# One block transpose for both heads, and row sums inverted by a power on GpSimd, in a four-layer attention kernel

## The chip, the core and the metric

The kernel runs on one core of a Trainium2 chip. The metric is the device time of one launch in microseconds (us), the median of several runs. One further execution was recorded by the hardware profiler; its trace gives the times of single instructions. The engines are PE (TensorE, matrix products), PEld (its weight loads), DVE (VectorE), ACT (ScalarE), POOL (GpSimd) and SP (SyncE, which here only issues DMAs). Each engine works through its own queue in order and waits on semaphores for the others.

## The reference

Two sequences of 1024 rows of 128 numbers run through eight residual blocks. Four of them are attention with 16 heads of 64, and they are what matters here:

```python
def attention(x):                        # x: (2, 1024, 128), after a layer norm
    s = q @ k.T / 8                      # per head, 1024 x 1024; three of the four are causal
    w = softmax(s, axis=-1)              # exp(s - rowmax) / rowsum
    return (w @ v) @ w_o
# layer a: one k and v for all heads, no mask;  b: causal;
# c: causal, k and v from a latent of 32;       d: causal, with biases
x = x + a(norm(x)); x = x + ffn(norm(x))
x = x + b(norm(x)); x = x + ffn(norm(x))
x = x + c(norm(x)); x = x + moe(norm(x))
x = x + d(norm(x)); x = x + moe(norm(x))
```

`ffn` is one dense product with its input rounded to a small grid, `moe` a small mixture of eight experts with two chosen for each row. Everything is float32.

## The kernel before, in words

A **unit** is one layer, one sequence and one pair of heads: 4 x 2 x 8 = 64 units. A unit is done in **steps**, each for one or two query tiles of 128 rows, chosen so that a step has at most 1024 columns of scores for each head. Layer a has no mask: eight steps, one query tile with 1024 keys each (`FULL_STEPS`, L587). The causal layers have five: query tiles 7, then 6 with 0, 5 with 1, 4 with 2, and 3 (`CAUSAL_STEPS`, L588). In all there are 128 + 3 x 80 = 368 steps.

For one step, in the order of the computation:

- `scores` (L623): PE multiplies queries by keys for both heads into PSUM (`sc`, two buffers, one for each head); DVE takes the negated row maximum of each head and query tile (`nmax`, L682).
- `exponentials` (L688): ACT writes exp(score - max) into the tile `pr` and the row sums into `tot` (L693). The tile `pr` has two buffers.
- `normalize` (L698): DVE takes the reciprocal of the row sums, one instruction of 128x2 or 128x4 (`rec`, L701). POOL multiplies the probabilities by it in place, one instruction for each head and query tile (L705).
- `transposes` (L761): the probabilities must be transposed for the product with the values. Most key tiles are transposed by DVE in 32x32 blocks, one instruction for each head and query tile (L775), into the tile `slots`. Key tiles outside a "blocked" range go through PE (`pp`, L792) and a copy on ACT (L793): in layer a the last key tile, in the others query tiles 0 to 3.
- `blocks_moved` (L736): when two neighbouring query tiles are done, the 32-partition blocks are moved to their places in `prT` by 16 DMAs issued on SP (L750). In layer a 13 are DMAs, two are copies on POOL (L754) and one a copy on ACT.
- `weigh` (L804): PE multiplies the transposed probabilities by the values (`av`, L849 and L844), ACT copies the result, PE multiplies by the output weights (`po`, L870), ACT copies it, and POOL adds it into x (L893).

The main loop (L1089) is a software pipeline written by hand; every engine gets its instructions in the order in which this loop emits them. In the iteration of step n it emits first the transposes of step n - 2. The normalising of step n - 1 is emitted after the first part of these transposes:

```python
            for _ in transposes(st):
                if last_step:
                    normalize(last_step.pop())
```

`transposes` is a generator, and a part ends at each `yield`. So DVE's queue before the change holds: transpose of head 0 (step n - 2), reciprocal (step n - 1), transpose of head 1 (step n - 2), then the maxima of step n. After that the iteration emits the additions into x, the scores, maxima and exponentials of step n, parts of the next unit's projections and of other work (layer norms, feed-forward blocks, as `side`), and four parts of `weigh`. A block of probabilities is used by `weigh` at the earliest two steps after its moves were emitted (L1131).

Where the tile `pr` lies in memory: before, it is [128, 2, 1024], so each head's columns are contiguous.

Of the kernel before, what the change touches and what calls it, by code (L numbers as in the profile page):

```python
# [9 lines left out]
F32 = mybir.dt.float32  # L10
BF16 = mybir.dt.bfloat16
I32 = mybir.dt.int32
AF = mybir.ActivationFunctionType
ALU = mybir.AluOpType
# [3 lines left out]
P = 128  # L18
B, S, D = 2, 1024, 128
NT = S // P  # L20
H, DH = 16, 64
NPAIR = H // 2
QB = 512
NQB = S // QB
# [3 lines left out]
TPA = AB // P  # L28
# [8 lines left out]
def kernel(ctx: ExitStack, tc: tile.TileContext, a: dict, out: bass.AP):  # L37
    nc = tc.nc

    const = ctx.enter_context(tc.tile_pool(name="const", bufs=1))  # L40
# [18 lines left out]
    for b in range(B):  # L59
        xb = xpool.tile([P, NT, D], F32, tag=f"x{b}", name=f"x{b}")  # L60
        for g in range(NT // TPB):
            nc.sync.dma_start(
                out=xb[:, g * TPB : (g + 1) * TPB, :],
# [42 lines left out]
    prT_four = probTp.tile([P, 2 * 4 * AB], F32, tag="prT_four", name="prT_four")  # L106
    latT_first = probTp.tile([P, S], F32, tag="latT", name="latT")


    stats = {}  # L110

# [149 lines left out]
    def moe_group(nm, b, g, last, xT, eng=nc.gpsimd, other=None):  # L261
# [3 lines left out]
        if other:  # L265
            xn = qkp.tile([P, TPB, D], F32, tag="qx", name=f"xn_{k}")
            hids = [
                probp.tile([P, 2, S], F32, tag="pr", name=f"hid_{k}_{n}").rearrange(
                    "p h (c q) -> p (h c) q", q=QB
                ) for n in range(2)  # L270
            ]
        else:
            xn = None
# [335 lines left out]
    def keys(u, qt):  # L609
        return qt + 1 if layers[u[0]]["causal"] else NT  # L610

    def step_of(u, qts):
        k = f"{tag_of(u)}_{qts[0]}"
        at = {}
        if len(qts) == 2:
            at = {qts[1]: 0, qts[0]: keys(u, qts[1]) * P}
        else:
            at = {qts[0]: QB - min(QB, keys(u, qts[0]) * P // 2)}
        pr = probp.tile([P, 2, S], F32, tag="pr", name=f"pr_{k}")
        tot = small.tile([P, 2, len(qts)], F32, tag="tot", name=f"tot_{k}")  # L620
        return dict(u=u, qts=qts, at=at, k=k, pr=pr, tot=tot)

    def scores(st):  # L623
# [61 lines left out]
            nmaxs.append(nmax)  # L685
        return sc, nmaxs

    def exponentials(st, h, sc, nmax):  # L688

        u, tot = st["u"], st["tot"]  # L690
        for n, qt in enumerate(st["qts"]):
            c = slice(st["at"][qt], st["at"][qt] + keys(u, qt) * P)
            nc.scalar.activation(  # L693
                st["pr"][:, h, c], sc[:, c], AF.Exp, bias=nmax[:, n : n + 1],
                accum_out=tot[:, h, n : n + 1],
            )

    def normalize(st):  # L698
        u, pr = st["u"], st["pr"]
        rec = small.tile([P, 2, len(st["qts"])], F32, tag="rec", name=f"rec_{st['k']}")  # L700
        nc.vector.reciprocal(out=rec, in_=st["tot"])  # L701
        for h in range(2):
            for n, qt in enumerate(st["qts"]):
                c = slice(st["at"][qt], st["at"][qt] + keys(u, qt) * P)
                nc.gpsimd.tensor_scalar(  # L705
                    out=pr[:, h, c], in0=pr[:, h, c], scalar1=rec[:, h, n : n + 1], scalar2=1.0,
                    op0=ALU.mult, op1=ALU.mult,
                )

# [26 lines left out]
    def blocks_moved(u, qb):  # L736


        t, src = prT_of(u, qb)[:, : 2 * blocked(u, qb) * AB], blocks_of(u, qb)
        n = src.shape[1] // 4  # L740
        def ends(i, r):
            return t[QUARTERS[r], i * n : (i + 1) * n], src[QUARTERS[i], r * n : (r + 1) * n]

        copied = (1, 2, 3) if layers[u[0]]["kind"] == "shared" else ()
        for i, r in MOVES:
            if i != r or i not in copied:
                o, x = ends(i, r)
                nc.sync.dma_start(out=o, in_=x)  # L750
        for i in copied:
            o, x = ends(i, i)
            if i < 3:
                nc.gpsimd.tensor_scalar(  # L754
                    out=o, in0=x, scalar1=1.0, scalar2=1.0, op0=ALU.mult, op1=ALU.mult
                )
            else:
                copies.append((o, x))
        probT[u, qb] = t.rearrange("p (i t h c) -> p t h i c", t=TPA, h=2, i=4)

    def transposes(st):  # L761

        u, pr = st["u"], st["pr"]
        for qt in st["qts"]:
            qb, cols = qt // TPA, slice(qt % TPA * P, (qt % TPA + 1) * P)
            nk, nb = keys(u, qt), blocked(u, qb)
            for h in range(2 if nb else 0):
                n = min(nk, nb)  # L770
                dst = blocks_of(u, qb).rearrange(
                    "p (r t h k q) -> p t h k r q", r=4, t=TPA, h=2, q=32
                )[:, qt % TPA, h, :n]
                src = pr[:, h, st["at"][qt] : st["at"][qt] + n * P]
                nc.vector.transpose(  # L775
                    dst,
                    src.rearrange("p (k r q) -> p k r q", r=4, q=32),
                )
                yield
            if nb < nk and nb:  # L780
                o = rest_of(u, qb)[:, qt % TPA].unsqueeze(2)
            elif nb < nk:
                if (u, qb) not in probT:
                    probT[u, qb] = prT_of(u, qb).rearrange("p (h k q) -> p h k q", h=2, q=AB)
                o = probT[u, qb][:, :, :, cols]
            for k0 in range(nb, nk, 2):
                k1 = min(k0 + 2, nk)
                pt = ps_m.tile([P, 2, 2, P], F32, tag="pm", name=f"pp_{tag_of(u)}_{qt}_{k0}")
                for h in range(2):
                    for kt in range(k0, k1):  # L790
                        c0 = st["at"][qt] + kt * P
                        nc.tensor.transpose(pt[:, h, kt - k0, :], pr[:, h, c0 : c0 + P], ident)  # L792
                nc.scalar.copy(o[:, :, k0 - nb : k1 - nb], pt[:, :, : k1 - k0, :])  # L793
                yield
            complete[u, qb] = complete.get((u, qb), 0) + 1
            if nb and complete[u, qb] == TPA:
                blocks_moved(u, qb)
# [6 lines left out]
    def weigh(u, qb, bank, kt, ends):  # L804


        li, b, p = u
        causal = layers[li]["causal"]
        nkt = keys(u, (qb + 1) * TPA - 1)
        n, nb = bank.index(qb), len(bank)  # L810
        if kt == 0 and n == 0:
            pv_of[u] = ps_av.tile([P, 2, AB], F32, tag="av", name=f"av_{tag_of(u)}_{qb}")
        av = pv_of[u]

        t0 = max(0, kt - qb * TPA) if causal else 0

        def moving(h, kt, t0, t1=TPA):
            if not blocked(u, qb):
                return probT[u, qb][:, h, kt, t0 * P : t1 * P]
            if kt >= blocked(u, qb):  # L820
                return rest_of(u, qb)[:, :, h]
            x = probT[u, qb][:, t0, h] if t1 - t0 == 1 else probT[u, qb][:, :, h]
            cols = slice(kt * 32, (kt + 1) * 32)
            return x[:, :, cols] if t1 - t0 == 1 else x[:, :, :, cols]

        def shaped(o, t0, t1=TPA):
            if not blocked(u, qb):
                return o[:, t0 * P : t1 * P]
            if kt >= blocked(u, qb):
                return o.rearrange("p (t q) -> p t q", t=TPA)  # L830
            if t1 - t0 == 1:
                return o[:, t0 * P : t1 * P].rearrange("p (i q) -> p i q", q=32)
            return o.rearrange("p (t i q) -> p t i q", t=TPA, q=32)

        for h in range(2):
            if layers[li]["kind"] == "latent":

                o = av[QUARTERS[2 * h + kt % 2], n]
                if kt == 1 and t0:
                    nc.tensor.matmul(  # L840
                        shaped(o, 0, t0), lhsT=zeros, rhs=moving(h, 0, 0, t0),
                        start=True, stop=True,
                    )
                nc.tensor.matmul(  # L844
                    shaped(o, t0), lhsT=vs[u][:, kt, :], rhs=moving(h, kt, t0), start=(kt < 2),
                    stop=(kt >= nkt - 2),
                )
            else:
                nc.tensor.matmul(  # L849
                    shaped(av[ROWS[h], n], t0), lhsT=vs[u][:, kt, h, :], rhs=moving(h, kt, t0),  # L850
                    start=(kt == 0), stop=(kt == nkt - 1),
                )
        if ends:
            o = attp.tile([P, 2, AB], F32, tag="at", name=f"attnT_{tag_of(u)}_{qb}")
            if layers[li]["kind"] == "bias":
                nc.scalar.activation(
                    o[:, :nb], av[:, :nb], AF.Identity, bias=b_v[:, p : p + 1]
                )
            else:
                nc.scalar.copy(o[:, :nb], av[:, :nb])  # L860
            outs.append((u, bank, o))
# [371 lines left out]
```

## Time and profile before

| what | value |
|---|---|
| time, median of 3 runs | 2314.12 us (2311.34 to 2315.66) |
| the profiled execution: span from its first to its last instruction | 2309.5 us |
| mean granted PE clock in it | 0.969 |
| instructions | 43436 |
| DVE block transposes (L775), count and length | 640; 0.83 us for 640 elements to 1.23 us for 1024 |
| DVE reciprocals (L701) | 368; 0.15 to 0.17 us |
| POOL normalising products (L705) | 1024; 0.38 us for 128 elements to 1.12 us for 1024 |
| layers a, b, c, d in the span | 24 to 690, 690 to 1188, 1188 to 1677, 1677 to 2235 us |
| one step of layer a, on average | 5.16 us |

The profiled execution has no time of its own beside its span; the runs' median is 4.6 us above that span.

How to read the lines that follow: a group or a timeline row names the source line, the engine and the operation, then output <- input with the name of the tile (`sc_a` is the scores of layer a). A row of waits names who waited for whom, the total in us, how many times, and the longest. A table of stretches gives, for each, its length and the busy time of PE, PEld, DVE, ACT and POOL with the number of instructions. The chain that ended last is followed back from the last instruction to what released it, step by step; its shares tell on which engine the time went along that chain.

### The profile page before, as it was taken

The page shows a single profiled execution, that of the slowest core. Times are in us where ns is not written, and L with a number is a line of the kernel's source. Part 1 is how long each engine was busy: PE and PEld are TensorE (multiplying, and loading weights), DVE is VectorE, ACT ScalarE, POOL GpSimd, SP SyncE. Part 2 cuts the span into 40 slices and gives each one's busy share as a digit, 9 for nine tenths or more (in the row PEclk, how much of TensorE's full clock was granted, in tenths as well). Part 3 has the DMA queues.
Part 4 walks back from the last instruction along what each step waited for, and adds up shares of the span by engine and source line. Part 5 has one row for each costly group of instructions (what it writes and reads, how often), then busy time and mean ns, then how long its engine had stood idle before and what let it go on. Part 6 is the DMA issues. An engine that isn't in the chain of part 4 may idle for free.

```text
span 2309.5 us, 43436 instructions
## 1 busy us (share of the span) xinstructions
PE 2112.7 (91%) x14833; PEld 1232.0 (53%) x14833; DVE 1716.0 (74%) x2695; ACT 1491.3 (65%) x3340; POOL 1285.7 (56%) x1723
## 2 busy tenths in 40 slices
PE   6999999999998999999987897888889999999986
PEld 2454444444445666666654454444455666656653
DVE  7978999999986876678668877776666566766544
ACT  5777777767765666666665566656666557666552
POOL 4756767767765454455545645555644446544441
PEclk9999999999999999999998889899899999999997
DMA  5666666556676666666655556544665546646450
GB/s 139 145 150 151 154 150 149 135 131 153 149 189 153 151 154 161 164 153 156 150 130 121 121 128 146 130 104 111 162 156 131 125 114 156 162 118 145 110 135 10
DMA packets 144635, 320.45 MB, mean 139 GB/s; under 512 B 48288, under 2 KB 58784, under 8 KB 144416
## 3 DMA queue, kind: packets, MB, share of 16 engines
q1 hardware_dynamic: 144416, 317.67, 58.2%
q8 instruction: 120, 1.97, 0.4%
q14 instruction: 99, 0.81, 0.1%
HBM read 10.27 MB, written 2.10 MB: 5 GB/s over the span
## 4 chain that ended last, share of the span: by engine, by line
PE 49%; DVE 15%; SPq 12%; ACT 10%; DMA 5%; issue 5%; POOL 3%; DVEq 0%; ACTq 0%; POOLq 0%
SPq L750 12%; PE sc_a L638 5%; PE av_a L849 4%; PE av_d L849 4%; DVE slots L775 4%; DMA prT<-slots 4%; PE sc_b L638 4%; PE av_b L849 4%; PE sc_d L638 4%; DVE nmax_a L682 3%; ACT pr_a L693 3%; ACT pr_c L693 3%; PE sc_c L638 3%; DVE nmax_d L682 2%; DVE nmax_c L682 2%
## 5 line engine op out<-in xcount | busy, mean ns | idle before, releaser
L693 ACT ACTIVATE pr_a<-sc_a,nmax_a 128x1024 f32<-128x1024 f32 x256 | 283.2, 1111 | 169.9 <-DVE nmax_a L682 168.0
L705 POOL TENSOR_SCALAR pr_a<-pr_a,rec_a 128x1024 f32<-128x1024 f32 x256 | 284.1, 1123 | 192.9 <-DVE rec_a L701 192.6
L705 POOL TENSOR_SCALAR pr_d<-pr_d,rec_d 128x1024 f32<-128x1024 f32 (+7 forms) x256 | 186.9, 750 | 269.0 <-DVE rec_d L701 268.8
L682 DVE TENSOR_REDUCE nmax_a<-sc_a 128x1 f32<-128x1024 f32 x256 | 298.3, 1204 | 28.0 <-PE sc_a L638 27.6
L705 POOL TENSOR_SCALAR pr_b<-pr_b,rec_b 128x1024 f32<-128x1024 f32 (+7 forms) x256 | 187.3, 752 | 219.9 <-DVE rec_b L701 219.5
L705 POOL TENSOR_SCALAR pr_c<-pr_c,rec_c 128x1024 f32<-128x1024 f32 (+7 forms) x256 | 187.5, 753 | 206.4 <-DVE rec_c L701 206.4
L682 DVE TENSOR_REDUCE nmax_d<-sc_d 128x1 f32<-128x1024 f32 (+7 forms) x256 | 177.1, 747 | 150.2 <-PE sc_d L644 150.2
L693 ACT ACTIVATE pr_c<-sc_c,nmax_c 128x1024 f32<-128x1024 f32 (+7 forms) x256 | 186.5, 739 | 153.5 <-DVE nmax_c L682 123.9
L693 ACT ACTIVATE pr_b<-sc_b,nmax_b 128x1024 f32<-128x1024 f32 (+7 forms) x256 | 186.5, 739 | 146.8 <-DVE nmax_b L682 130.3
L638 PE MATMUL sc_a<-k_a,q_a 64*128 64x512 f32 x512 | 266.8, 631 | 15.0 <-ACT pr_a L693 14.2
L775 DVE STREAM_TRANSPOSE slots<-pr_a 128x896 f32<-128x896 f32 x256 | 278.8, 1093 | 1.7 <-DMA prT<-slots 1.3
L693 ACT ACTIVATE pr_d<-sc_d,nmax_d 128x1024 f32<-128x1024 f32 (+7 forms) x256 | 186.6, 739 | 135.0 <-DVE nmax_d L682 129.5
L638 PE MATMUL sc_a<-k_a,qx_a 64*128 64x512 f32 x512 | 264.1, 631 | 0.0
L682 DVE TENSOR_REDUCE nmax_b<-sc_b 128x1 f32<-128x1024 f32 (+7 forms) x256 | 176.6, 745 | 89.0 <-PE sc_b L644 88.9
L682 DVE TENSOR_REDUCE nmax_c<-sc_c 128x1 f32<-128x1024 f32 (+7 forms) x256 | 176.8, 747 | 84.8 <-PE sc_c L653 84.0
L849 PE MATMUL av_a<-prT,v_a 128*64 128x256 f32 x1792 | 221.4, 386 | 7.5 <-DMA prT<-slots 5.2
L849 PEld LDWEIGHTS av_a<-prT,v_a 128*64 128x64 f32 x1792 | 121.1, 136 | 122.3 <-issue 69.0
L638 PE MATMUL sc_d<-k_d,q_d 64*128 64x512 f32 (+3 forms) x416 | 159.9, 497 | 0.3 <-ACT pr_d L693 0.3
L638 PE MATMUL sc_b<-k_b,q_b 64*128 64x512 f32 (+3 forms) x416 | 159.1, 495 | 1.1 <-ACT pr_b L693 1.1
L638 PE MATMUL sc_d<-kx_d,qx_d 64*128 64x512 f32 (+3 forms) x416 | 154.3, 490 | 0.2
L638 PE MATMUL sc_b<-kx_b,qx_b 64*128 64x512 f32 (+3 forms) x416 | 153.5, 488 | 0.7 <-ACT pr_b L693 0.6
L775 DVE STREAM_TRANSPOSE slots<-pr_b 128x1024 f32<-128x1024 f32 (+3 forms) x128 | 130.5, 1024 | 9.6 <-DMA prT<-slots 9.0
(408 smaller groups left out, 4782.3 us busy)
## 6 DMA issues: line engine op xcount, KB each, us to landing
prT<-slots SPq DMA_DIRECT2D x768, 128.0 KB, 2.3
prT<-slots SPq DMA_DIRECT2D x832, 112.0 KB, 2.2
prT<-slots SPq DMA_DIRECT2D x768, 96.0 KB, 2.1
qx_b<-q_b SPq DMA_DIRECT2D x32, 256.0 KB, 3.5
kx_b<-k_b SPq DMA_DIRECT2D x32, 256.0 KB, 3.4
qx_d<-q_d SPq DMA_DIRECT2D x32, 256.0 KB, 3.6
kx_d<-k_d SPq DMA_DIRECT2D x32, 256.0 KB, 3.5
x<-in_x SPq DMA_DIRECT2D x4, 256.0 KB, 3.7
```

Source lines behind the costliest of these rows:

```text
L638: yield nc.tensor.matmul(sc[h][:, at[qt] + k0 : at[qt] + k1], lhsT=q[r, qt * P : (qt + 1) * P], rhs=kk[r, k0:k1], start=True, stop=not dia ...
L682: nc.vector.tensor_reduce(out=nmax[:, n : n + 1], in_=sc[h][:, c], axis=AX.X, op=ALU.max, negate=True)
L693: nc.scalar.activation(st["pr"][:, h, c], sc[:, c], AF.Exp, bias=nmax[:, n : n + 1], accum_out=tot[:, h, n : n + 1],)
L705: nc.gpsimd.tensor_scalar(out=pr[:, h, c], in0=pr[:, h, c], scalar1=rec[:, h, n : n + 1], scalar2=1.0, op0=ALU.mult, op1=ALU.mult,)
L750: nc.sync.dma_start(out=o, in_=x)
L775: nc.vector.transpose(dst, src.rearrange("p (k r q) -> p k r q", r=4, q=32),)
L849: nc.tensor.matmul(shaped(av[ROWS[h], n], t0), lhsT=vs[u][:, kt, h, :], rhs=moving(h, kt, t0), start=(kt == 0), stop=(kt == nkt - 1),)
```

## The change

Three edits go together.

1. The tile `pr` becomes [128, 8, 2, 128]: key tile by key tile, head 0 and head 1 in turn. An exponential or a normalising product of one head now writes or reads rows of 128 elements with gaps of 128.
2. With both heads of a key tile side by side, one DVE transpose does a query tile for both heads: 320 transposes of twice the size in place of 640. The order of the blocks within `slots` and `prT` becomes key tile, head instead of head, key tile; the moves and their sizes stay.
3. The reciprocal on DVE goes. POOL computes `tot` to the power -1 with a two-operand instruction (the exponents are a tile of -1.0 set once at the start), directly ahead of its normalising products. It waits for ACT's row sums itself.

```diff
+    minus = const.tile([P, 4], F32, tag="minus", name="minus")
+    nc.gpsimd.memset(minus, -1.0)
...
-        pr = probp.tile([P, 2, S], F32, tag="pr", name=f"pr_{k}")
+        pr = probp.tile([P, NT, 2, P], F32, tag="pr", name=f"pr_{k}")
...
+    def tiles_of(st, qt):
+        t0 = st["at"][qt] // P
+        return st["pr"][:, t0 : t0 + keys(st["u"], qt)]
+
...
             nc.scalar.activation(
-                st["pr"][:, h, c], sc[:, c], AF.Exp, bias=nmax[:, n : n + 1],
-                accum_out=tot[:, h, n : n + 1],
+                tiles_of(st, qt)[:, :, h, :], sc[:, c].rearrange("p (k q) -> p k q", q=P),
+                AF.Exp, bias=nmax[:, n : n + 1], accum_out=tot[:, h, n : n + 1],
             )
...
     def normalize(st):
-        u, pr = st["u"], st["pr"]
         rec = small.tile([P, 2, len(st["qts"])], F32, tag="rec", name=f"rec_{st['k']}")
-        nc.vector.reciprocal(out=rec, in_=st["tot"])
+        nc.gpsimd.tensor_tensor(
+            out=rec, in0=st["tot"],
+            in1=minus[:, : 2 * len(st["qts"])].rearrange("p (h n) -> p h n", h=2), op=ALU.pow,
+        )
         for h in range(2):
             for n, qt in enumerate(st["qts"]):
-                c = slice(st["at"][qt], st["at"][qt] + keys(u, qt) * P)
+                pt = tiles_of(st, qt)[:, :, h, :]
                 nc.gpsimd.tensor_scalar(
-                    out=pr[:, h, c], in0=pr[:, h, c], scalar1=rec[:, h, n : n + 1], scalar2=1.0,
+                    out=pt, in0=pt, scalar1=rec[:, h, n : n + 1], scalar2=1.0,
                     op0=ALU.mult, op1=ALU.mult,
                 )
...
-            for h in range(2 if nb else 0):
+            tiles = tiles_of(st, qt)
+            if nb:
                 n = min(nk, nb)
                 dst = blocks_of(u, qb).rearrange(
-                    "p (r t h k q) -> p t h k r q", r=4, t=TPA, h=2, q=32
-                )[:, qt % TPA, h, :n]
-                src = pr[:, h, st["at"][qt] : st["at"][qt] + n * P]
+                    "p (r t c q) -> p t c r q", r=4, t=TPA, q=32
+                )[:, qt % TPA, : 2 * n]
                 nc.vector.transpose(
                     dst,
-                    src.rearrange("p (k r q) -> p k r q", r=4, q=32),
+                    tiles[:, :n].rearrange("p k h (r q) -> p (k h) r q", q=32),
                 )
                 yield
```

The other lines of the diff only follow the new order of the blocks: the view of `prT` in `blocks_moved`, the columns that PE's transposes and `weigh` read, and two scratch tiles of the last feed-forward block that share the buffers of `pr`.

More of the change, by code (lines that the diff above doesn't have):

```diff
@@ L267, in moe_group @@
             hids = [
-                probp.tile([P, 2, S], F32, tag="pr", name=f"hid_{k}_{n}").rearrange(
-                    "p h (c q) -> p (h c) q", q=QB
+                probp.tile([P, NT, 2, P], F32, tag="pr", name=f"hid_{k}_{n}").rearrange(
+                    "p (c n) h q -> p c (n h q)", c=2 * NQB
                 ) for n in range(2)
@@ L758, in blocks_moved @@
                 copies.append((o, x))
-        probT[u, qb] = t.rearrange("p (i t h c) -> p t h i c", t=TPA, h=2, i=4)
+        probT[u, qb] = t.rearrange("p (i t k h q) -> p t h i k q", t=TPA, h=2, i=4, q=32)
     def transposes(st):
-        u, pr = st["u"], st["pr"]
+        u = st["u"]
         for qt in st["qts"]:
@@ L790, in transposes @@
                     for kt in range(k0, k1):
-                        c0 = st["at"][qt] + kt * P
-                        nc.tensor.transpose(pt[:, h, kt - k0, :], pr[:, h, c0 : c0 + P], ident)
+                        nc.tensor.transpose(pt[:, h, kt - k0, :], tiles[:, kt, h, :], ident)
                 nc.scalar.copy(o[:, :, k0 - nb : k1 - nb], pt[:, :, : k1 - k0, :])
@@ L822, in moving @@
             x = probT[u, qb][:, t0, h] if t1 - t0 == 1 else probT[u, qb][:, :, h]
-            cols = slice(kt * 32, (kt + 1) * 32)
-            return x[:, :, cols] if t1 - t0 == 1 else x[:, :, :, cols]
+            return x[:, :, kt] if t1 - t0 == 1 else x[:, :, :, kt]
         def shaped(o, t0, t1=TPA):
```

## The prediction

> **What bounds the kernel now.** First the page's busy times and the chain that ended last, to see which engine the end hangs on; then the four layers apart, since they have different limits.
>
> ```profile
> PE 2112.7 (91%) x14833; PEld 1232.0 (53%) x14833; DVE 1716.0 (74%) x2695; ACT 1491.3 (65%) x3340; POOL 1285.7 (56%) x1723
> PE 49%; DVE 15%; SPq 12%; ACT 10%; DMA 5%; issue 5%; POOL 3%; DVEq 0%; ACTq 0%; POOLq 0%
> 24.00:690.00 666.00, 632.21 (x3719) 302.84 (x3719) 604.05 (x741) 489.59 (x880) 459.63 (x478) 0.99 0.63 148
> 690.00:1188.00 498.00, 475.49 (x3626) 318.55 (x3626) 354.77 (x597) 321.78 (x806) 260.07 (x393) 0.99 0.65 153
> 1188.00:1677.00 489.00, 411.44 (x3328) 227.69 (x3327) 360.65 (x612) 303.06 (x772) 271.47 (x410) 0.91 0.55 128
> 1677.00:2235.00 558.00, 529.39 (x3870) 345.88 (x3871) 355.22 (x607) 351.20 (x842) 274.23 (x405) 0.99 0.57 137
> ```
>
> The last four lines are the layers a, b, c, d (stretch, its length, then busy PE, PEld, DVE, ACT, POOL and the granted clock). The third column is what matters: PE is busy 95% of layers a, b and d, and 84% of c. PE's idle time is 34, 23, 78 and 29 us, 163 in all, and nothing that happens on VectorE (DVE) can win more than its share of that. DVE is near its own limit only in a (604 of 666).
>
> So the question is which idle time of PE ends on something that DVE holds up. The view of waits, by layer and for PE, gives these lines (waited for, us, times, longest), layer a first, then b, c and d:
>
> ```profile
> PE sc_a L638 <- ACT pr_a L693: 14.2, 23, 1.7
> PE pp_a L792 <- POOL pr_a L705: 5.8, 12, 0.8
> PE av_a L849 <- DMA prT<-slots: 5.2, 7, 0.9
> PE av_b L849 <- DMA prT<-slots: 5.4, 5, 2.9
> PE sc_c L638 <- ACT pr_c L693: 22.0, 43, 0.9
> PE pp_c L792 <- POOL pr_c L705: 20.6, 26, 2.7
> PE av_c L844 <- DMA prT<-slots: 9.7, 5, 2.7
> PE av_d L849 <- DMA prT<-slots: 7.6, 4, 4.8
> ```
>
> Last, one step of layer a on DVE and POOL, from the timeline (start, length, engine, line; in brackets the idle time before):
>
> ```profile
> 326.79 1.10 DVE L775 STREAM_TRANSPOSE slots<-pr_a 128x896 f32<-128x896 f32 x1
> ...
> 328.17 0.17 DVE L701 RECIPROCAL rec_a<-tot_a 128x2 f32<-128x2 f32 x1 [0.28 <-ACT pr_a L693]
> 328.25 1.09 DVE L775 STREAM_TRANSPOSE slots<-pr_a 128x896 f32<-128x896 f32 x1
> ...
> 328.51 2.22 POOL L705 TENSOR_SCALAR pr_a<-pr_a,rec_a 128x1024 f32<-128x1024 f32 x2 [0.88 <-DVE rec_a L701]
> ```
>
> Between the two transposes of an older step DVE stands still until the newest step's exponentials are done, because the reciprocal is queued there. Behind it wait the second transpose and, at 329.27, the maxima whose scores PE had ready at about 328.6.
>
> **What goes from DVE.** (1) Half of the 640 transposes. 640 elements take 0.827 us and 1024 take 1.225: 1.036 ns an element and 0.164 us fixed. The merged one has the same elements, so 320 x 0.164 = 52 us go. (2) All 368 reciprocals, by their rows 57.9 us. (3) The idle time before them: 28.4 in a, 35.4, 35.3 and 30.8 in the others, 130 us. Together 240 us of DVE's time, nearly all beside a busy PE. What is late next is PE itself.
>
> **What POOL takes on.** 368 powers of 128x2 or 128x4 elements, each ahead of its own normalising, and the waits for the exponentials. No power is in this trace. From below it can't beat POOL's smallest two-operand row, 128x8 in 0.204 us (L142). From above I take a plain product of 128x512 in 1.27 us (L883): more than a hundred times the elements. I take p = 0.4, nearest to the small row, doubled for the longer arithmetic. That is 147 us on POOL, which then has 1433 busy. Queued behind each power are the two or four normalising products, POOL's copies of blocks (L754) and the additions into x; the next transposes and PE's pp wait for the products. From the end of the exponentials to the start of the products it takes 0.30 us now (the reciprocal and two hops, 0.25 more than a direct wait), so products start p - 0.25 = 0.15 us later where the reciprocal was punctual, and earlier where it was late.
>
> **What merely changes its pattern.** The exponentials write rows of 128 with gaps. ACT's copies of 128x512 into strided blocks (L793, 592 ns) cost what those into plain tiles do (L877, 586), so nothing. The products on POOL read and write such rows: L328 writes 32 elements in four strided rows in 291 ns, where the line through 128 and 1024 elements (0.378 and 1.123 us) gives 0.298. Again nothing. The moves, PE's moving operands and their strides stay. Merging makes a transpose wait for both heads' products instead of one: in the step above they end at 330.7, the next transposes start at 331.51, so 0.8 us of cover, 0.65 with the power; past that DVE would stand there. The memset of the exponents runs once, in the prologue.
>
> [...]
>
> **The sum, p = 0.4.** Layer a: DVE reaches the maxima 0.164 + 0.155 + 28.4/128 = 0.54 us sooner per step. 23 waits of PE for exponentials, 0.62 on average, lose 0.54 each: 12.4. The blocks' moves and the copies behind the exponentials (5.2 and 4.3 us of PE waits, 7 times each) gain as much per wait, 7.6; half of it I expect to come back as another wait: 3.8. Lost: 12 waits of pp x 0.15 = 1.8. Net 14.4.
>
> Causal layers: a step's second transpose ends about 1.0 us sooner (1382.66 in c becomes 1379.67 + 2 x 1.09 - 0.16 = 1381.69), and the 16 moves behind it start sooner. Of the waits of av for moves: b 4 of 5.4, c 5 of 9.7, d 3 of 7.6. In c also the waits of pp for POOL: in four places (around 1242, 1274, 1304 and 1556) the reciprocal sat behind DVE's other work 1.0 to 2.6 us after its exponentials. They hold 9.5 us of PE idle; I take 8. In the regular unit of c the reciprocal is punctual and pp waits for the products once a unit, so 16 x 0.15 = 2.4 are lost. sc_c <- ACT stays: scores, maxima and exponentials wait for each other in a ring there. Net b 4, c 10.6, d 3.
>
> 14.4 + 4 + 10.6 + 3 = **32 us**. The profiled execution spans 2309.5 us; the runs' median is 2314.1, 4.6 more for what lies around a span. Applied to the median: 2282 us.
>
> With p = 0.2: a loses nothing and c gains 0.8 instead of losing 2.4, so 37 us, 2277. With p = 1.27: the pp waits of a cost 12, those of c 16, so a 4, c -3, b and d 7: 8 us, 2306.
>
> **Rivals.** (1) DVE's time doesn't reach the end. PE is 95% busy, its waits for exponentials pass to the next in line (moves, whose queue on SP issues 13 of 0.59 us per two steps of a, 7.7 of 10.3 us). For it: DVE holds only 15% of the chain. Against: 216 of a's 256 maxima don't wait for PE, so DVE sets their time. Then 0 to 8 us are won: 2310. (2) POOL becomes the bound; this ends slower. In a, two steps hold four products of 1.123, two copies of 0.936 and half an addition of 1.28: 7.0 of 10.3 us. Anything over (10.3 - 7.0)/2 = 1.65 us more per step, by the power or by slower products, decides. At 2.0 us a costs 64 x 0.7 = 45, c 16 x 1.75 = 28 less its 13, b and d still win 7: 53 us more, 2367. For it: 368 powers of unknown price. Against: two to four elements a partition. (3) The power costs about 1.3 us and eats the gain: 2306, as above. That the edit doesn't do what it says I exclude: every reciprocal and half the transposes leave DVE's queue in the code.
>
> **Numbers.** Forecast 0.57; rival 1 0.15; rival 2 0.21; rival 3 0.07. A change under 0.2% (4.6 us) can't be told from none. Faster: 0.57 + 0.05 + 0.04 = 0.66; same: 0.09 of rival 1 and 0.03 of 3, 0.12; slower: 0.21 and the rest of 1, 0.22. The range goes from 2256, where three fifths (58) of the 95 us of PE waits named here would be won, to 2345, halfway into rival 2; some 1 in 10 is left out on each side. The forecast's own range is 2262 to 2303.
>
> **What would show it.** Right: 320 transposes of about 2.02 us for 1792 elements; no DVE idle before a reciprocal; POOL's pow row at 0.2 to 0.6 us; PE idle in a near 20 us, c near 67; sc_a <- ACT at a few us. Wrong: a pow row over 1 us; products over 1.2 us for 1024; transposes or pp waiting for POOL by tens of us; POOL over 95% of layer a; or PE's idle time unchanged under other names.

## The result, and the profile after

The changed kernel takes **2330.04 us** (median of 4 runs, 2328.50 to 2331.34) against 2312.73 us for the kernel before (4 runs). The ratio is 1.0068, with a 95% interval of [1.0048, 1.0088] (the two medians alone give 1.0075): it is slower by 0.7%, where 2282 us and a gain had been forecast. The profiled execution spans 2327.0 us, 17.5 us more than that of before, at a mean granted clock of 0.963.

The page's busy times and the shares of the chain that ended last, of the changed kernel:

```profile
PE 2129.7 (92%) x14833; PEld 1237.7 (53%) x14833; DVE 1666.4 (72%) x2007; ACT 1492.2 (64%) x3340; POOL 1597.0 (69%) x2092
PE 52%; POOL 15%; DVE 9%; issue 7%; SPq 7%; ACT 6%; DMA 3%; DVEq 0%; POOLq 0%; ACTq 0%
```

DVE got its relief, and its share of the chain went from 15% to 9%. But POOL is busy 311 us longer, and its share of the chain went from 3% to 15%: 12 points more, where DVE gave up 6. PE's idle time over the whole span is what it was, 197.3 us (before 196.8), so the 17.5 us stand in its busy time.

The four layers of the changed kernel (stretch, length, then busy PE, PEld, DVE, ACT, POOL and the granted clock). Each stretch runs from a layer's first row maximum to the next layer's, that of d to its last:

```profile
22.60:690.10 667.50, 629.85 (x3697) 303.44 (x3697) 582.75 (x483) 488.65 (x875) 549.90 (x604) 0.99 0.65 148
690.10:1185.50 495.40, 476.22 (x3647) 318.10 (x3644) 345.58 (x453) 322.01 (x806) 333.29 (x473) 1.00 0.66 155
1185.50:1687.00 501.50, 424.99 (x3306) 232.12 (x3307) 351.43 (x468) 303.14 (x773) 345.74 (x490) 0.89 0.54 124
1687.00:2243.80 556.80, 532.05 (x3877) 344.77 (x3875) 344.76 (x464) 351.19 (x837) 342.16 (x481) 0.99 0.58 136
```

Cut at the same marks, the kernel before has 663.6, 498.4, 489.6 and 552.8 us. So a lost 3.9, b won 3.0, c lost 11.9, d lost 4.0, and the tail and head 0.7. Two profiles of one and the same kernel (e3_merge and e3_again below) differ by 4 us in b and under 2 in a, c and d, so b says nothing here and d little. In c the loss doesn't stand in PE's idle time (76.5 us, before 80.2), but in its busy time (425.0, before 409.4) and its clock (0.89, before 0.91).

The new power and the normalising products, from POOL's groups of the changed kernel (line, operation, count, busy us and mean ns, idle time before them and what ended it):

```profile
L714 POOL TENSOR_SCALAR pr_a<-pr_a,rec_a 128x1024 f32<-128x1024 f32 x256 | 284.6, 1124 | 13.0
...
L707 POOL TENSOR_TENSOR rec_a<-tot_a,minus 128x2 f32<-128x2 f32 x128 | 91.5, 715 | 91.9 <-ACT pr_a L700 56.2 <-PE av_a L856 20.6 <-PE sc_a L641 4.3
...
L707 POOL TENSOR_TENSOR rec_c<-tot_c,minus 128x4 f32<-128x4 f32 x48 | 49.4, 1030 | 88.7 <-ACT pr_c L700 88.7
```

A power takes 0.715 us for two elements a partition and 1.03 for four, 0.84 on average over the 368 steps; 0.4 had been assumed. The products over strided rows cost what the plain ones did (1124 ns, before 1123).

PE's waits in the changed kernel (waited for, us, times, longest):

```profile
PE pp_c L800 <- POOL pr_c L714: 30.2, 32, 3.5
PE sc_c L641 <- ACT pr_c L700: 24.6, 40, 1.7
PE sc_a L641 <- ACT pr_a L700: 15.2, 17, 2.0
PE pp_a L800 <- POOL pr_a L714: 14.0, 22, 1.9
```

pp waits for POOL 17.8 us longer than before in a and c together (5.8 and 20.6 then), and since PE's idle time is the same, other waits are shorter by about as much (av_c for the moves went from 9.7 to 1.2, for one). The wait that was to vanish, sc_a for the exponentials, is still there (14.2 before). And DVE now waits for POOL in front of its transposes, which it hardly did before (2.1 us, in c):

```profile
DVE slots L784 <- POOL pr_a L714: 23.5, 33, 2.7
...
DVE slots L784 <- POOL pr_c L714: 17.4, 14, 4.3
...
DVE slots L784 <- POOL pr_d L714: 14.2, 17, 4.3
```

One step of layer a shows how this comes about: the timeline of the changed kernel, ACT, POOL and DVE (start, length, engine, line; in brackets the idle time before).

```profile
308.25 1.93 POOL L763 TENSOR_SCALAR prT<-slots 32x896 f32<-32x896 f32 x2
309.05 0.20 ACT L700 ACTIVATION_READ_ACCUMULATOR pr_a<-sc_a,nmax_a 128x1 f32 x1
310.26 0.71 POOL L707 TENSOR_TENSOR rec_a<-tot_a,minus 128x2 f32<-128x2 f32 x1
...
311.07 2.22 POOL L714 TENSOR_SCALAR pr_a<-pr_a,rec_a 128x1024 f32<-128x1024 f32 x2
...
313.33 2.05 DVE L784 STREAM_TRANSPOSE slots<-pr_a 128x1792 f32<-128x1792 f32 x1 [0.59 <-POOL pr_a L714]
```

The row sums are there at 309.25. POOL copies blocks until 310.18, then computes the power, then both heads' products until 313.29, and only then can the one transpose for both heads begin. From 308.25 to 313.29 POOL has no gap of more than 0.1 us: 5.04 us in a step of 5.2. Over the whole of a it is busy only 82% of the time, and it even stands idle 91.9 us in front of the powers. The power doesn't slow DVE's own instructions: a merged transpose of layer a takes 2037 ns on average here and 2033 in e1 below, which has no power.

### The profile page after: what moved, and what is told of

Same layout as the page of the kernel before. It is cut to its first block, busy times and chain, and to the rows that moved or that the text cites. A ratio compares the mean times of both kernels' runs of the same rounds, so it can differ in the third digit from the quotient of the medians.

```text
span 2327.0 us, 43762 instructions
## 1 busy us (share of the span) xinstructions
PE 2129.7 (92%) x14833; PEld 1237.7 (53%) x14833; DVE 1666.4 (72%) x2007; ACT 1492.2 (64%) x3340; POOL 1597.0 (69%) x2092
## 4 chain that ended last, share of the span: by engine, by line
PE 52%; POOL 15%; DVE 9%; issue 7%; SPq 7%; ACT 6%; DMA 3%; DVEq 0%; POOLq 0%; ACTq 0%
SPq L759 7%; PE sc_a L641 6%; PE av_d L856 5%; PE av_a L856 4%; PE sc_b L641 4%; PE av_b L856 4%; PE sc_d L641 4%; POOL pr_a L714 3%; POOL pr_c L714 3%; ACT pr_c L700 2%; DMA prT<-slots 2%; PE sc_c L641 2%; DVE nmax_d L685 2%; DVE slots L784 2%; PE pp_d L800 2%
## 5 line engine op out<-in xcount | busy, mean ns | idle before, releaser
L700 ACT ACTIVATE pr_a<-sc_a,nmax_a 128x1024 f32<-128x1024 f32 x256 | 283.2, 1111 | 172.0 <-DVE nmax_a L685 169.6
L714 POOL TENSOR_SCALAR pr_a<-pr_a,rec_a 128x1024 f32<-128x1024 f32 x256 | 284.6, 1124 | 13.0
L641 PE MATMUL sc_a<-k_a,q_a 64*128 64x512 f32 x512 | 265.3, 631 | 15.2 <-ACT pr_a L700 14.9
L784 DVE STREAM_TRANSPOSE slots<-pr_a 128x1792 f32<-128x1792 f32 x128 | 260.8, 2037 | 25.5 <-POOL pr_a L714 23.5
L707 POOL TENSOR_TENSOR rec_d<-tot_d,minus 128x4 f32<-128x4 f32 (+1 forms) x80 | 71.7, 896 | 192.0 <-ACT pr_d L700 184.4
L707 POOL TENSOR_TENSOR rec_b<-tot_b,minus 128x4 f32<-128x4 f32 (+1 forms) x80 | 73.2, 915 | 141.7 <-ACT pr_b L700 140.0
L707 POOL TENSOR_TENSOR rec_c<-tot_c,minus 128x4 f32<-128x4 f32 (+1 forms) x80 | 72.9, 911 | 136.7 <-ACT pr_c L700 119.8
```

Source lines behind the costliest of these rows:

```text
L641: yield nc.tensor.matmul(sc[h][:, at[qt] + k0 : at[qt] + k1], lhsT=q[r, qt * P : (qt + 1) * P], rhs=kk[r, k0:k1], start=True, stop=not dia ...
L700: nc.scalar.activation(tiles_of(st, qt)[:, :, h, :], sc[:, c].rearrange("p (k q) -> p k q", q=P), AF.Exp, bias=nmax[:, n : n + 1], accum_o ...
L707: nc.gpsimd.tensor_tensor(out=rec, in0=st["tot"], in1=minus[:, : 2 * len(st["qts"])].rearrange("p (h n) -> p h n", h=2), op=ALU.pow,)
L714: nc.gpsimd.tensor_scalar(out=pt, in0=pt, scalar1=rec[:, h, n : n + 1], scalar2=1.0, op0=ALU.mult, op1=ALU.mult,)
L784: nc.vector.transpose(dst, tiles[:, :n].rearrange("p k h (r q) -> p (k h) r q", q=32),)
```

## The experiments

Two theories stood against each other first. **P**: the power's price on POOL eats a gain that is really there. **M**: merging is to blame, because one transpose now waits for the products of both heads, or because the strided rows cost time. Then, within P, **L** (latency: the power lies between the row sums and the products, and all that follows starts later) against **O** (occupancy: POOL's queue is full in places, wherever the power stands). All ratios are to the kernel before, run beside each experiment on the same chip; its medians there were 2313.55, 2312.98, 2314.13 and 2312.94 us.

| run | median us | ratio [95%] |
|---|---|---|
| the change | 2330.04 | 1.0068 [1.0048, 1.0088] |
| e1_mult: a product in the power's place | 2295.39 | 0.9928 [0.9912, 0.9943] |
| e2_pow: the power alone | 2320.13 | 1.0029 [1.0017, 1.0040] |
| e3_merge: the merge alone | 2294.47 | 0.9920 [0.9905, 0.9936] |
| e3_again: the same once more | 2296.65 | 0.9920 [0.9906, 0.9934] |
| e6_twice: the power twice | 2386.19 | 1.0317 [1.0297, 1.0337] |
| x3_layout: the layout alone | 2313.25 | 1.0002 [0.9988, 1.0015] |
| x4_behind: e1 with the power behind the products | 2314.32 | 1.0009 [0.9996, 1.0022] |
| x1_change_nocopy: the change, two copies off POOL | 2335.28 | 1.0099 [1.0079, 1.0119] |
| x2_merge_nocopy: e3 with the same | 2310.32 | 0.9992 [0.9978, 1.0006] |
| y1_uneven: e3, transpose cut 5 + 2 in layer a | 2292.87 | 0.9902 [0.9887, 0.9917] |
| z2_two: e1 with two small products | 2304.49 | 0.9964 [0.9951, 0.9976] |
| z1_turned: e1, c's second head first | 2295.03 | 0.9925 [0.9909, 0.9941] |

### e1_mult, e2_pow, e3_merge: which part costs

e1_mult, against the changed kernel:

```diff
-            in1=minus[:, : 2 * len(st["qts"])].rearrange("p (h n) -> p h n", h=2), op=ALU.pow,
+            in1=minus[:, : 2 * len(st["qts"])].rearrange("p (h n) -> p h n", h=2), op=ALU.mult,
```

> The changed kernel with the power replaced by a plain product of the row sums and the constants, so the probabilities are multiplied by minus their row sum instead of divided by it; all else is the change. Two theories. P: the price of the power (0.72 us for 128x2, 1.03 for 128x4 in the changed kernel's trace) puts POOL on the ring exponentials, products, transposes, maxima. M: the merging is to blame, because a transpose now waits for both heads' products and the rows of one head have gaps. P expects the product at about 0.20 us and the sum that the prediction gave for p = 0.2: 2277 us, at most 2290, with DVE and PE hardly waiting for POOL in layer a. M expects no change from the changed kernel: 2320 to 2335 us.

e2_pow, against the kernel before:

```diff
-        nc.vector.reciprocal(out=rec, in_=st["tot"])
+        nc.gpsimd.tensor_tensor(
+            out=rec, in0=st["tot"],
+            in1=minus[:, : 2 * len(st["qts"])].rearrange("p (h n) -> p h n", h=2), op=ALU.pow,
+        )
```

> The power alone: the kernel before, with its two transposes and its layout, but the reciprocals as a power on POOL. P expects it slower than before, as slow as the change or slower, 2320 to 2345 us, with the power rows at 0.72 and 1.03 us. M expects it faster than before, 2285 to 2305 us, since DVE gets 58 us of reciprocals and 130 us of idle time back.

e3_merge takes the same edit back in the changed kernel:

```diff
-        nc.gpsimd.tensor_tensor(
-            out=rec, in0=st["tot"],
-            in1=minus[:, : 2 * len(st["qts"])].rearrange("p (h n) -> p h n", h=2), op=ALU.pow,
-        )
+        nc.vector.reciprocal(out=rec, in_=st["tot"])
```

> The merging alone: the new layout and one transpose for both heads, with the reciprocal on DVE at its old place in the program, which is now behind the whole merged transpose. P expects it faster than before, 2285 to 2305 us: 52 us of fixed costs go from DVE, and in the causal layers, where a pair of exponentials takes longer than the transpose, the reciprocal is still punctual; in layer a it comes some 0.6 us late, so a wins little. M expects it slower than before, 2320 to 2335 us.

M falls as the whole cause: with the merge and a cheap reciprocal on either engine the kernel is 0.7 to 0.8% faster. P holds: the power alone, without the merge, makes the kernel slower. The difference between the change and e1 is one operation code, and 35 us of span (2327.0 and 2292.3), of which 14.2 are in a, 14.5 in c and 4.6 in d; 19.7 of them are idle time of PE and 15.0 its busy time, beside mean granted clocks of 0.963 and 0.968; whether late products or something else lowers the clock isn't shown. But e1 lies 5 us above the 2290 us that P allowed at most, so a part of P's gain isn't there.

The two halves don't add, either. The merge alone wins 0.8% and the power alone loses 0.3%, but together they lose 0.7%: once the power is there, the merge costs some 9 us (0.39%, from e2 to the change, and the two intervals don't overlap). M's wait shows where. In e2, where a transpose needs the products of one head only, DVE waited little for them in a:

```profile
DVE slots L781 <- POOL pr_a L711: 4.3, 6, 1.6
```

In the change it is 23.5 us, 33 times (above). With the merge but without the power it is 4.3 us in e1 and 8.2 in e3. In c and d it is 7.7 and 5.1 us in e2, 17.4 and 14.2 in the change. So each half alone leaves this wait short, and late products delay the one transpose that needs both heads. That the 9 us come from this wait is read from these rows; no run isolates it.

In e3 the reciprocal stands in DVE's queue behind one whole transpose of 2.04 us. Its group among DVE's of e3, for layer a (before, 28.4 us of idle time stood in front of these 128 reciprocals):

```profile
L707 DVE RECIPROCAL rec_a<-tot_a 128x2 f32<-128x2 f32 x128 | 15.7, 123 | 0.7 <-ACT pr_a L700 0.7
```

By the time the long transpose ends, the row sums have long been there, and 0.7 us of idle time is left. Over all layers DVE's waits in front of the reciprocals went from 130 to 30 us. PE's waits in e3:

```profile
PE pp_c L797 <- POOL pr_c L711: 26.2, 25, 3.5
PE pp_a L797 <- POOL pr_a L711: 22.6, 32, 1.3
PE sc_c L641 <- ACT pr_c L700: 20.2, 41, 1.1
```

and those in e1:

```profile
PE sc_c L641 <- ACT pr_c L700: 26.7, 43, 2.2
PE sc_a L641 <- ACT pr_a L700: 16.8, 19, 2.2
PE pp_c L800 <- POOL pr_c L714: 15.9, 22, 2.5
...
PE pp_a L800 <- POOL pr_a L714: 4.4, 8, 0.8
```

e1 and e3 reach about the same time by different ways. In e3 the maxima come early and the products late: sc_a waits 1.7 us, pp_a 22.6. In e1 it is the reverse.

### e6_twice, z2_two: what a microsecond on POOL costs

e6_twice computes the power a second time, into a tile of its own, ahead of the products of the changed kernel:

```diff
+        nc.gpsimd.tensor_tensor(
+            out=twice, in0=st["tot"],
+            in1=minus[:, : 2 * len(st["qts"])].rearrange("p (h n) -> p h n", h=2), op=ALU.pow,
+        )
```

> The changed kernel with every power computed twice, the second into a tile that nobody reads: one more instruction of 0.72 or 1.03 us on POOL per step. P expects layer a to reach POOL's limit (two steps need 7.0 + 4 x 0.72 = 9.9 us of 10.4) and c to pay about 1 us more for each of its 16 units: 2355 to 2400 us. M expects 2325 to 2340 us.

z2_two, against e1_mult:

```diff
+        nc.gpsimd.tensor_tensor(
+            out=rec, in0=rec,
+            in1=minus[:, : 2 * len(st["qts"])].rearrange("p (h n) -> p h n", h=2), op=ALU.mult,
+        )
```

> The price that the prediction assumed: e1_mult with a second product behind the first (row sum times minus one twice, so the probabilities are multiplied by their row sum), about 0.4 us per step in the power's place. The prediction's sum for p = 0.4 says 2282 us. A straight line through e1_mult (0.21 us per step on average, 2295) and the change (0.84, 2330) says 2306. If the price alone was wrong, the first; if the gain and the slope were wrong too, the second.

z2's 2304.49 us lie at the second of its two forecasts, so the gain and the slope were wrong too; e6's 2386.19 lie in P's range. With e1 and the change this gives four points of one curve; the price is POOL's busy time in these groups, divided by 368 steps:

| price per step, us | ratio | us won (-) or lost, ratio x 2313 |
|---|---|---|
| 0.21 (e1) | 0.9928 | -16.7 |
| 0.41 (z2) | 0.9964 | -8.3 |
| 0.84 (the change) | 1.0068 | +15.7 |
| 1.66 (e6) | 1.0317 | +73.3 |

Between the points a microsecond more per step costs 41, 56 and 70 us: increments count from the first. That each later one costs more is likely, but not shown for the first three points: with the intervals of the ratios the slopes are about 41 ± 23, 56 ± 13 and 70 ± 8. A straight line between the middle points crosses nought at about 0.56 us.

### x3_layout: do the strided rows cost?

Against e3_merge, so with the reciprocal on DVE, between the two transposes again:

```diff
-            if nb:
+            for h in range(2 if nb else 0):
...
-                )[:, qt % TPA, : 2 * n]
+                )[:, qt % TPA, h, :n]
...
-                    tiles[:, :n].rearrange("p k h (r q) -> p (k h) r q", q=32),
+                    tiles[:, :n, h, :].rearrange("p k (r q) -> p k r q", q=32),
```

> The new layout alone: two transposes per query tile as before, the reciprocal between them on DVE as before, but the rows of one head with gaps for ACT, POOL, DVE and PE. If the pattern costs nothing, as the rows of single instructions say, and e3_merge's gain is that of the merging: 2308 to 2318 us, no difference from before. If the gain comes from the layout: 2290 to 2300 us.

1.0002 [0.9988, 1.0015]: the new layout with two transposes costs nothing and wins nothing. So what e3 wins is the merge's, with what comes with it: e3's reciprocals stand behind the whole transpose and not between two. In x3 DVE still waits 129 us in front of them, in e3 30.

### x4_behind: latency or occupancy?

Against e1_mult, behind the normalising products:

```diff
+        behind = small.tile([P, 2, len(st["qts"])], F32, tag="behind", name=f"behind_{st['k']}")
+        nc.gpsimd.tensor_tensor(
+            out=behind, in0=st["tot"],
+            in1=minus[:, : 2 * len(st["qts"])].rearrange("p (h n) -> p h n", h=2), op=ALU.pow,
+        )
```

> As e1_mult (a plain product in the power's place, so the probabilities are multiplied by minus their row sum), with the power behind the normalising products, its result unread. POOL does all that it does in the change and 0.2 us more per step; only the way from the exponentials to the products is short again. Theory L: what costs is the power's latency on the ring from the exponentials over the products to the transposes. Theory O: what costs is POOL's occupancy, since its queue then is late for everything. L expects 2293 to 2303 us as in e1_mult; O expects 2325 to 2340 as in the change.

Layers a and c of e1:

```profile
23.20:676.50 653.30, 623.63 (x3697) 301.09 (x3698) 577.83 (x483) 488.40 (x876) 483.99 (x605) 0.99 0.66 151
...
1172.90:1659.90 487.00, 417.99 (x3306) 228.70 (x3307) 349.02 (x469) 302.46 (x773) 289.59 (x491) 0.90 0.56 128
```

and of x4_behind:

```profile
23.30:691.10 667.80, 629.03 (x3697) 303.84 (x3697) 582.65 (x482) 488.14 (x875) 569.64 (x731) 0.99 0.63 147
...
1190.30:1678.20 487.90, 412.20 (x3306) 226.72 (x3307) 349.85 (x469) 302.29 (x773) 359.57 (x571) 0.91 0.54 128
```

The 2314.32 us lie between the two forecasts, and each theory is right in one layer. In a the power costs as much behind the products as in front of them (667.8 and 667.5 us, against 653.3 without it): O. POOL's queue is full around the block copies, and whatever stands in it pushes the next step's products, for which transposes and pp wait (17.6 and 10.3 us in a of x4, 4.3 and 4.4 in e1). O need not be all of a's 14 us, since x4 has the small product beside the power and so 20 us more on POOL in a than the change; from e1 to z2, 24 us more there cost 4.3 us (653.3 to 657.6), so some 4 us can be L. In c the power behind the products costs 0.9 us, in front of them 14.5: L. There POOL has gaps (88.7 us in front of the 48 larger powers of the change), and what counts is the way from the row sums through the products and pp to the next scores. d points the same way as c (553.3 behind, 556.8 in front, 552.2 without), by little more than the 1.8 us between two profiles of one kernel.

### x1_change_nocopy, x2_merge_nocopy: POOL without the block copies

The same edit in the changed kernel (x1) and in e3_merge (x2):

```diff
-        copied = (1, 2, 3) if layers[u[0]]["kind"] == "shared" else ()
+        copied = (3,) if layers[u[0]]["kind"] == "shared" else ()
```

> The changed kernel with layer a's two block copies taken from POOL and moved by SP's DMAs instead (15 per block, not 13): POOL has 1.87 us less per two steps in layer a, the ring stays as it is. O expects layer a to come back to about 655 us and the whole to 2312 to 2318 us. L expects a within 4 us of the change's 667.5 and the whole at 2323 to 2332 us. The other layers stay in both.

> The control for x1_change_nocopy, and a candidate for a faster kernel: merging alone with the reciprocal on DVE, with the two block copies moved by SP's DMAs. POOL isn't full there (460 of 658 us in a). L and O both expect e3_merge's 2294 us, from 2 us less (the products start earlier behind the copies) to 8 us more (two further DMA issues of 0.59 us before a block has landed).

Handing the two copies to SP's DMAs was to empty POOL's queue in a. Both runs are slower than either theory allowed (2335.28 against at most 2332, 2310.32 against at most 2302). What became late instead is the moves themselves, 960 of 112 KB in place of 832, which the control shows, since there is no power in it: av_a waited 4.3 us for them in e3. PE's longest wait in x1:

```profile
PE av_a L856 <- DMA prT<-slots: 35.9, 28, 2.4
```

and in x2, the control:

```profile
PE av_a L853 <- DMA prT<-slots: 32.5, 31, 1.9
```

Layer a went to 675.4 us in x1 and 671.4 in x2. With the copies gone from POOL the change costs 4.0 us more than the merge alone in a, with them 9.4 (667.5 and 658.1). That fits O, but another bound lies over both kernels, so it proves little.

### y1_uneven, e3_again: can the merge's gain be had with earlier products?

y1_uneven, against e3_merge; e3_again has no edit, and runs beside it:

```diff
-                nc.vector.transpose(
-                    dst,
-                    tiles[:, :n].rearrange("p k h (r q) -> p (k h) r q", q=32),
-                )
-                yield
+                cuts = [0, n] if layers[u[0]]["causal"] else [0, 5, n]
+                for k0, k1 in zip(cuts, cuts[1:]):
+                    nc.vector.transpose(
+                        dst[:, 2 * k0 : 2 * k1],
+                        tiles[:, k0:k1].rearrange("p k h (r q) -> p (k h) r q", q=32),
+                    )
+                    yield
```

> A candidate: e3_merge (merging, reciprocal on DVE), but in layer a the merged transpose is cut in two, five key tiles and then two, with the reciprocal between them. The first piece takes 1280 x 1.036 ns + 0.164 = 1.49 us, about as long as the second head's exponential and its sum need behind the maxima (1.35 us), so the reciprocal comes about 0.5 us sooner than behind the whole transpose and DVE doesn't stand still; the second cut costs 0.164 us per step. If the late reciprocal holds layer a back (pp_a waits 22.6 us for POOL in e3_merge), a falls from 658 to about 652 and the whole to 2286 to 2291 us. If DVE's length of a step holds it back (4.45 us between reciprocals where PE is ahead), a is 658 to 664 and the whole 2294 to 2301.

> e3_merge once more, beside y1_uneven on one chip: 2294 us, 0.8% below before, if the first measurement holds.

The reciprocal now comes after five of seven key tiles. pp_a's waits for POOL fell from 22.6 us in e3 to 15.2, those of sc_a rose from 1.7 to 8.3, and the sum stayed (24.3 and 23.5). Layer a took 660.0 us and the whole 2292.87, between the two forecasts, so the run doesn't say which cause holds a back. 0.9902 [0.9887, 0.9917] and 0.9920 [0.9906, 0.9934] overlap. Either is the best kernel of this study, some 0.8 to 1% faster than the one before.

### z1_turned: why PE is busy longer in c

In c the score products of the two heads run side by side where both can start: in the step at 1314.23 below, the first four records, of 0.59 to 0.69 us, start within 0.02 us. PE's timeline of the changed kernel shows two steps of 1024 columns a head:

```profile
1314.23 1.14 PE L641 MATMUL sc_c<-latT,q_c 32*128 32x384 f32 x12
...
1318.60 1.13 PE L641 MATMUL sc_c<-latT,q_c 32*128 32x256 f32 x4 [0.56 <-ACT pr_c L700]
1319.94 1.13 PE L641 MATMUL sc_c<-latT,q_c 32*128 32x256 f32 x8 [0.21 <-ACT pr_c L700]
```

Twelve products take 1.14 us when both heads' PSUM tiles are free. Where these come free one after the other (both later rows waited for ACT's exponentials), four start alone and the rest follow, and the same number takes 2.26 us in the two rows. PE counts as busy for all of that. Over c the score products with their masks take 152.3 us before, 161.6 in the change, 159.8 in e1 and 148.9 in e3. z1 emits the second head first, to see whether the order makes the split:

```diff
-            in_turn([half(h) for h in range(2) for half in (lower, upper)])
+            in_turn([half(h) for h in (1, 0) for half in (lower, upper)])
```

> e1_mult with the score products of layer c issued for the second head first, whose buffer comes free last, so that all four products start together and run side by side instead of one head after the other. If PE's busy time in c is only stretched by products that run in two turns (159.8 us for sc_c in e1_mult against 150.9 before, 487 us for the layer), sc_c falls below 150 us, PE's idle time in c rises by about as much, and the layer stays within 4 us. If those products were work that PE can't be spared, c gets shorter by some 9 us.

They still take 157.2 us, c 485.4 (487.0 in e1), and the time is that of e1. The split remained, so the run decides nothing. Nor does the price on POOL set this time: x3, as fast as the kernel before, has 157.7 us, and e6, with the power twice, 155.4, less than the change. What sets it stays open; that products wait in it for ACT one head at a time is read from the rows above.

## Why the prediction was wrong

**The frame was right.** PE's waits set what a cheaper DVE can win: in the change DVE's busy time fell by 50 us and the 130 us of waits in front of the reciprocals went altogether, yet no version won more than 23 us. **The gain from DVE per step of a was somewhat too large, and wrong in its parts.** 0.54 us were forecast. In the prediction's step, two transposes and the reciprocal hold DVE from 326.79 us to the maxima at 329.27, 2.48. In e1 the merged transpose holds it 1.95, 0.53 less:

```profile
297.97 2.04 DVE L784 STREAM_TRANSPOSE slots<-pr_a 128x1792 f32<-128x1792 f32 x1
299.92 2.32 DVE L685 TENSOR_REDUCE nmax_a<-sc_a 128x1 f32<-128x1024 f32 x2
```

But not every step had idle time in front of its reciprocal (97 of 128 had): the starts of the two transposes lie 1.46 us apart in the prediction's step and 1.37 on average over the layer, so on average some 0.43 went. And the records overlap at their ends. The second transpose of that step, of 1.09 us, is followed after 1.02, so merging itself saves 0.07 to 0.09, not 0.164, and the reciprocal held 0.08 (328.17 to 328.25), not 0.155. The idle time in front of the reciprocal is most of it.

**The first failing step is the price p = 0.4 "nearest to the small row".** It is 0.84 on average. The bounds 0.204 and 1.27 held it. By the prediction's own slope of about 28 us per microsecond the error costs 12 us, which leaves a gain of 20; it can't turn the sign alone. Nothing in the trace gave this value: it was the row of another operation, doubled.

**The second, larger one is the sum at a given price.** e1 stands at p = 0.21, where 37 us were forecast, and wins 16.7; z2 stands at p = 0.41, where 32 were forecast, and wins 8.3. So of the 48 us between the forecast (-32) and the result (+15.7), 24 were missing at the assumed price already, and 24 came with the real one: 12 by the forecast's slope, 12 because the slope was too flat. Its terms, one by one:

- *"23 waits of PE for exponentials lose 0.54 each: 12.4."* They lost nothing: sc_a for ACT 14.2 us before, 16.8 in e1, 16.0 in z2. DVE came earlier and then waited for PE's scores instead: its maxima of a waited 27.6 us for them before, 57.9 in e1. That points to a ring through PE where this term saw a wait on DVE. Only e3, which delays the products, took the wait away, and gave it back at pp_a.
- *Moves and copies, 3.8 in a:* right. av_a went from 5.2 to 3.3 and po_a from 4.5 to 1.4, 5.0 together. In c 5 of 9.7 were forecast, 6.4 won in z2 (8.5 in the change). In b and d 4 and 3 were forecast; 1.5 and 1.7 came (8.0 to 6.5 and 7.6 to 5.9 in z2, over the whole span).
- *Late reciprocals in c, 8 less 2.4:* pp_c's waits fell from 20.6 to 19.5 in z2, 1.1 instead of 5.6. In the change they rose to 30.2.
- *PE's busy time as a constant:* never written as a term, and it took most of c's gain away. In z2 c's idle time fell by 10.1 us, nearly the forecast 10.6, but pp gave 1.1 of it and not 5.6. But its busy time rose by 6.3, half of it in the score products (152.3 to 155.4). In the change it rose by 15.6, 9.3 of it in these products, and the granted clock fell from 0.91 to 0.89. In x3 it rose by 7.2 with no power and no merge, so not all of this is the change's; its cause stays open.

**Rival 2 had most of the mechanism and the wrong threshold.** POOL did become what others wait for, and in a by occupancy, as it said. It put the turning point at 1.65 us per step, from an average: 7.0 of 10.3 us in use. Work on POOL comes in bunches, though. In the step shown, copies, power and products fill 5.04 of 5.2 us, and the next step has 0.8 us of idle time. From e1 to the change, 0.51 us more on each of 128 steps is 66 us of POOL's time in a, and 14.2 of them reached the end with POOL at 82%. Rival 3 expected 1.27 us to leave a gain of 8; 0.84 lost 15.7.

**The cover of 0.65 us for the merged transpose** was read from a step without copies ahead of the products. In 33 of 128 steps of a there was none, 23.5 us; with e1's small product 5 times, 4.3. The merge was counted as a gain whatever the power cost; beside the real power it lost 9 us (e2 to the change).

**The patterns cost nothing,** as said (x3, 1.0002). For POOL the prediction had one short row (L328, 32 elements in 291 ns). The changed kernel's long products settle it: 1124 ns for 1024 elements over rows of 128, before 1123, and ACT's exponentials into such rows take 1111 ns in both kernels.

Of what was to show it right, 320 transposes were there, those of 1792 elements 2.04 us long; of what was to show it wrong, transposes and pp waiting for POOL by tens of microseconds, a power of over 1 us (for 128x4), and PE's idle time unchanged under other names, 196.8 us before and 197.3 after.

## What to carry to other kernels

An engine that is busy 70 or 80% on average, as POOL was here (69% of the span, 82% of layer a), can have no slack where its work is bunched (5.04 of 5.2 us in the step shown): before moving an instruction onto it, read a timeline of the fullest step and ask what waits behind. An operation that the trace doesn't show should be priced over its whole range, and where the forecast's sign depends on it, the break-even price belongs beside the forecast. Two edits that are forecast together should also be priced apart, since one can need what the other takes: here the transpose for two heads needed early products. Alone it was worth 0.8%, and taking a 0.16 us reciprocal from the engine that did it cheaply cost all of that and more.

## What the runs showed of the hardware

- GpSimd's power of two tensors took 0.71 to 0.74 us for 128x2 and 1.02 to 1.03 for 128x4 in the change, so some 0.40 to 0.45 us and 0.15 more for each element a partition, an estimate from these two sizes; a product of the same shapes took 0.20 to 0.23 in e1, nearly the same for both.
- DVE's records overlap at their ends by some 0.08 us: a transpose of 1.09 us was followed by the next instruction after 1.02 (328.25 to 329.27 in the kernel before). Busy time summed from durations overstated what goes with an instruction here: 0.155 us for a reciprocal that held DVE for 0.08, and 0.164 for a merge that saves 0.07 to 0.09.
- PE's busy time for one and the same set of products isn't fixed: 148.9 to 161.6 us for the 1088 score and mask products of layer c, in e3 and in the change, beside granted clocks of 0.92 and 0.89. Twelve of them took 1.14 us started together and 2.26 started apart (four, then eight); how much of the difference comes from this, and how much from the clock, isn't shown.
